# Pair products of 32 fields: stores of three pairs in 12 KB rows, weights in whole 128-partition blocks of six pairs

## The chip, the cores and the metric

One core of one Trainium2 chip. The metric is the device time of one execution in microseconds (us), taken from several runs; the profile is of one execution, and its span is about 1.8 us shorter than that execution's time (768.7 us for the profiled one of the kernel before, 2 us above the median). The times of the kernels told here may be compared.

## The reference

For every pair of fields i < j (496 pairs of 32 fields) the row of field i goes through the pair's own 128x128 matrix and is multiplied by the row of field j:

```python
v_i = inputs[:, I_IDX, :]                            # 1024 x 496 x 128, fp32
v_j = inputs[:, J_IDX, :]
transformed = jnp.einsum('bpd,ped->bpe', v_i, W)     # W: 496 x 128 x 128
return transformed * v_j                             # 1024 x 496 x 128 = 260 MB
```

## The kernel before

Embedding lies on the 128 partitions and the batch of 1024 along the row; the host transposes. A "half-pair" is 512 columns of one pair. TensorE makes its product in PSUM: one fp32 matmul for the first 15 pairs, three matmuls of split operands (h, l, d) for the rest, with ScalarE scaling PSUM between them. ScalarE and GpSimd split weights and x. VectorE multiplies PSUM by field j into an output tile. SyncE issues nearly all transfers, loads and stores, in the order of the program.

```python
WL = 8          # pairs in one block of weights
OG = 2          # pairs in one output tile, and in one store
rpool = ctx.enter_context(tc.tile_pool(name="wr", bufs=3))   # raw weights, 4 KB a partition
opool = ctx.enter_context(tc.tile_pool(name="o", bufs=4))    # output, 8 KB a partition
...
def load_w(c, half, splits=(0, WL)):
    ...
        nc.sync.dma_start(out=w_raw[c][half::2, a:b, :], in_=wt[c, half, :, a:b, :])
...
def second(u):                                   # of half-pair u = 2 q + h
    ...
    g, k = divmod(q, OG)
    if k == 0 and h == 0:
        ots[g] = opool.tile([P, OG, BT], F32, tag="ot", name=f"ot_{g}")
    nc.vector.tensor_tensor(ots[g][:, k, s], po.pop(u), x_sb[j][:, s], ALU.mult)
    if q >= NQ - 2:
        nc.sync.dma_start(out=out[g, :, k, s], in_=ots[g][:, k, s])
    elif k == OG - 1 and h == 1:
        nc.sync.dma_start(out=out[g], in_=ots[g])

for u in range(2 * NQ + LAG):
    q = u // 2
    if u % (2 * WL) == 4 and (q // WL + 2) * WL < NQ:
        load_w(q // WL + 2, 1)                   # every second partition of a block
    if u % (2 * WL) == 12 and (q // WL + 3) * WL < NQ:
        load_w(q // WL + 3, 0)                   # the other ones, four pairs later
    ...
```

What matters later: the weights go out as two transfers of 64 partitions each (4 packets for each of the 16 DMA engines), four pairs apart, with two stores between them.

Of the kernel before, what the change touches and what calls it, by code (L numbers as in the profile page):

```python
# [7 lines left out]
F32 = mybir.dt.float32  # L8
# [3 lines left out]
P = 128  # L12
NF = 32
NQ = NF * (NF - 1) // 2
BT = 1024
HB = 512
WC = 2
WL = 8
OG = 2
EPS = 2.0**-12  # L20
NATIVE = 5
SHARED = 10
XDLAG = 10
LAG = 3
XLEAD = 5


def _pairs():

    return [(i, j) for i in range(NF - 2, -1, -1) for j in range(i + 1, NF)]  # L30


@with_exitstack
def kernel(
    ctx: ExitStack,
    tc: tile.TileContext,
    xt: bass.AP,
    wt: bass.AP,
    out: bass.AP,
):  # L40
















    nc = tc.nc
    pairs = _pairs()
    nchunk = NQ // WC

    xpool = ctx.enter_context(tc.tile_pool(name="x", bufs=1))
    spool = ctx.enter_context(tc.tile_pool(name="xs", bufs=2))
    rpool = ctx.enter_context(tc.tile_pool(name="wr", bufs=3))
    wpool = ctx.enter_context(tc.tile_pool(name="ws", bufs=4))
    opool = ctx.enter_context(tc.tile_pool(name="o", bufs=4))
    ppool = ctx.enter_context(tc.tile_pool(name="ps", bufs=8, space=bass.MemoryType.PSUM))

    x_sb = {}

    def load_x(f, n=1, pieces=1, eng=None):  # L70

        t = xpool.tile([P, n, BT], F32, tag=f"x{f}", name=f"x_{f}")
        s = BT // pieces
        for k in range(pieces):
            (eng or nc.sync).dma_start(out=t[:, :, k * s : (k + 1) * s], in_=xt[:, f : f + n, k * s : (k + 1) * s])
        for k in range(n):
            x_sb[f + k] = t[:, k, :]

    w_raw = {}

    def load_w(c, half, splits=(0, WL)):

        if c not in w_raw:
            w_raw[c] = rpool.tile([P, WL, P], F32, tag="w", name=f"w_{c}")
        for a, b in zip(splits, splits[1:]):
            nc.sync.dma_start(out=w_raw[c][half::2, a:b, :], in_=wt[c, half, :, a:b, :])

    w_s = {}

    def split_w(c, u):  # L90

        k = c * WC % WL
        raw = w_raw[c * WC // WL][:, k : k + WC, :].rearrange("p q e -> p (q e)")
        h, l, d = [wpool.tile([P, WC * P], F32R, tag=t, name=f"{t}_{c}") for t in ("wh", "wl", "wd")]
        nc.scalar.mul(h, raw, 1.0 - 2.0**-13)  # L95
        nc.gpsimd.tensor_tensor(l, raw, h.bitcast(F32), ALU.subtract)  # L96
        nc.gpsimd.tensor_scalar(d, h.bitcast(F32), EPS, 1.0, ALU.mult, ALU.mult)  # L97
        nc.gpsimd.tensor_tensor(d, l.bitcast(F32), d.bitcast(F32), ALU.subtract)  # L98
        w_s[c] = (h, l, d)

    x_s = {}
    later = []

    def split_x(f, a, u):

        if a == 0:
            x_s[f] = [spool.tile([P, BT], F32R, tag=t, name=f"{t}_{f}") for t in ("xh", "xl", "xd")]
        s = slice(a, a + HB)
        h, l, d = [t[:, s] for t in x_s[f]]
        nc.scalar.mul(h, x_sb[f][:, s], 1.0 - 2.0**-13)  # L110
        nc.gpsimd.tensor_tensor(l, x_sb[f][:, s], h.bitcast(F32), ALU.subtract)  # L111
        nc.gpsimd.tensor_scalar(l, l.bitcast(F32), 1.0 / EPS, 1.0, ALU.mult, ALU.mult)  # L112
        if f > NF - 2 - NATIVE - SHARED:
            later.append((min(u + XDLAG, 2 * first_q[f] + LAG - 1), d, h.bitcast(F32), l.bitcast(F32)))
        else:
            nc.gpsimd.tensor_tensor(d, h.bitcast(F32), l.bitcast(F32), ALU.subtract)  # L116

    nq0 = NATIVE * (NATIVE + 1) // 2
    c0 = nq0 // WC
    first_q = {i: q for q, (i, j) in reversed(list(enumerate(pairs)))}  # L120



    todo = []
    for c in range(c0, nchunk):
        todo.append(((c - 3) * WC + 1, max(c * WC, nq0), lambda u, c=c: split_w(c, u)))
    for i in range(NF - 2 - NATIVE, -1, -1):
        for a in range(0, BT, HB):
            todo.append((first_q[i + 1] + 1 if i < NF - 3 - NATIVE else 2, first_q[i], lambda u, i=i, a=a: split_x(i, a, u)))
    todo.sort(key=lambda t: t[1])  # L130

    load_w(0, 0, (0, 1))
    load_w(0, 1, (0, 1))
    load_w(0, 0, (1, WL))
    load_w(0, 1, (1, WL))
    load_x(NF - 2, pieces=2, eng=nc.scalar)
    load_x(NF - 1, pieces=2, eng=nc.scalar)
    load_x(NF - 3)
    load_x(NF - 4)
    load_w(1, 0)  # L140
    for f in range(NF - 5, NF - 4 - XLEAD, -1):
        load_x(f)
    load_w(1, 1)
    load_w(2, 0)


    ctx.enter_context(tc.manual_schedule())
    po, ots = {}, {}


    def first(u):
        q, h = divmod(u, 2)
        i, c = pairs[q][0], q // WC
        r = slice(q % WC * P, (q % WC + 1) * P)
        s = slice(h * HB, (h + 1) * HB)
        po[u] = ppool.tile([P, HB], F32, tag="po", name=f"po_{u}")
        if q < nq0:
            nc.tensor.matmul(po[u], w_raw[q // WL][:, q % WL, :], x_sb[i][:, s], start=True, stop=True)  # L158
        else:
            for t in (0, 1):  # L160
                nc.tensor.matmul(po[u], w_s[c][t][:, r], x_s[i][t][:, s], start=t == 0, stop=t == 1)  # L161
            nc.scalar.mul(po[u], po[u], 1.0 + EPS)  # L162

    def second(u):
        q, h = divmod(u, 2)
        i, j = pairs[q]
        r = slice(q % WC * P, (q % WC + 1) * P)
        s = slice(h * HB, (h + 1) * HB)
        if q >= nq0:
            nc.tensor.matmul(  # L170
                po[u], w_s[q // WC][2][:, r], x_s[i][2][:, s], start=False, stop=True, skip_group_check=True
# [4 lines that stand above are left out]
        nc.vector.tensor_tensor(ots[g][:, k, s], po.pop(u), x_sb[j][:, s], ALU.mult)  # L176
        if q >= NQ - 2:
            nc.sync.dma_start(out=out[g, :, k, s], in_=ots[g][:, k, s])
        elif k == OG - 1 and h == 1:
            nc.sync.dma_start(out=out[g], in_=ots[g])  # L180

    for u in range(2 * NQ + LAG):
        q = u // 2
        if u % (2 * WL) == 4 and (q // WL + 2) * WL < NQ:
            load_w(q // WL + 2, 1)
        if u % (2 * WL) == 12 and (q // WL + 3) * WL < NQ:
            load_w(q // WL + 3, 0)
        if u < 2 * NQ:
            i, j = pairs[q]
            if u % 2 == 0 and j == i + 1 and 0 <= i - 2 - XLEAD:  # L190
                load_x(i - 2 - XLEAD)
            first(u)
        if u >= LAG:
            second(u - LAG)
        if u % 2 == 1:
            ready = [t for t in todo if t[0] <= q]
            if ready:
                ready[0][2](u)
                todo.remove(ready[0])
        while later and later[0][0] <= u:  # L200
            nc.vector.tensor_tensor(*later.pop(0)[1:], ALU.subtract)  # L201
    assert not todo and not later
# [27 lines left out]
```

## Time and profile before

| | before |
|---|---|
| time, median of 3 runs | 766.5 us (765.69 to 768.17) |
| SyncE's queue | 50,544 packets, 98.9% of 16 engines' span |
| stores / weight loads / x loads on that queue | 251 / 126 / 30 transfers |
| TensorE, the next busiest | 93% |

The lines behind this are in the prediction. The kernel is bound by DMA, so the account is one of a DMA engine's time, worked out from the packet records of the trace and averaged over the 16 engines:

- *net*: for each size of packet, the count times the median duration, less the 3 ns by which a packet overlaps its follower;
- *stalls*: what packets took above the median of their size, for stores and for loads apart;
- *gaps*: time between packets in which the engine had none; *rest*: fetches of instructions (2.2 to 2.5), the start, the run-out and the lag of the slowest engine.

Before: 726.0 net + 14.2 stalls of stores + 10.4 of loads + 7.1 gaps + 9.1 rest = 766.8, the span. A *ring* is here the queue that one issuing engine (SyncE or ScalarE) fills; *landing* is the last of a transfer's sixteen semaphore updates.

### The profile page before, as it was taken

How to read it: one execution, taken by the hardware profiler on the slowest of the kernel's cores; microseconds unless marked ns; L12 is line 12 of the kernel's file. 1: busy time of each engine (PE TensorE's matmuls, PEld its weight loads, DVE VectorE, ACT ScalarE, POOL GpSimd, SP SyncE). 2: the span in 40 equal slices, each digit the busy share in tenths (PEclk: the TensorE clock that was granted, in tenths of full speed). 3: DMA queues.
4: the chain of work that ended last, by engine and by line, in shares of the span. 5: the costliest groups of instructions: out<-in, count | busy, mean ns of one | idle time of the engine just before them, and what ended most of it. 6: DMA issues, size and time to landing. Idle time of an engine off the chain costs nothing.

```text
span 766.8 us, 11879 instructions
## 1 busy us (share of the span) xinstructions
PE 715.1 (93%) x2946; PEld 547.0 (71%) x2946; DVE 631.9 (82%) x1012; ACT 634.0 (83%) x1256; POOL 594.8 (78%) x863
## 2 busy tenths in 40 slices
PE   6997999999999998999999989999999999999994
PEld 2475776677767676777776768787878777777773
DVE  3878988898877787887787878888888888888895
ACT  2186988888888898888888989998989899999893
POOL 1687998879889878878788786979787879696660
PEclk9999999999999999999999999999999999999997
DMA  9999999999999999999999999999999999999997
GB/s 341 397 419 406 414 406 385 412 397 410 415 407 409 409 393 413 410 414 413 392 424 408 401 398 405 418 414 418 418 419 421 413 408 416 410 410 411 409 399 294
DMA packets 51189, 310.12 MB, mean 404 GB/s; under 512 B 6576, under 2 KB 6704, under 8 KB 19504
## 3 DMA queue, kind: packets, MB, share of 16 engines
q1 hardware_dynamic: 50544, 308.31, 98.9%
q10 hardware_dynamic: 576, 1.05, 0.4%
q8 instruction: 24, 0.39, 0.2%
q14 instruction: 45, 0.37, 0.1%
HBM read 49.28 MB, written 260.05 MB: 403 GB/s over the span
## 4 chain that ended last, share of the span: by engine, by line
DMA 45%; PE 33%; DVE 17%; issue 2%; POOL 1%; DVEq 0%; ACT 0%; ACTq 0%; POOLq 0%
DMA out_dram<-ot 44%; PE po L161 21%; DVE ot L176 16%; PE po L170 10%; PE po L158 2%; DVE xd L201 2%; DMA x<-in_xt_dram 1%; POOL xd L116 0%; POOL xl L111 0%; POOL wl L96 0%; DVEq L176 0%; POOL wd L98 0%; POOL xl L112 0%; ACT wh L95 0%; POOL wd L97 0%
## 5 line engine op out<-in xcount | busy, mean ns | idle before, releaser
L176 DVE TENSOR_TENSOR ot<-po,x 128x512 f32<-128x512 f32 x992 | 618.6, 684 | 126.0 <-DMA out_dram<-ot 76.3
L162 ACT ACTIVATE po<-po 128x512 f32<-128x512 f32 x962 | 550.5, 583 | 103.8 <-PE po L161 56.2
L161 PE MATMUL po<-xh,wh 128*128 128x512 f32 x962 | 386.8, 402 | 26.0 <-DVE ot L176 25.0
L170 PE MATMUL po<-xd,wd 128*128 128x512 f32 x962 | 377.0, 392 | 5.4 <-DVE xd L201 4.5
L161 PE MATMUL po<-xl,wl 128*128 128x512 f32 x962 | 377.8, 393 | 3.4 <-POOL wl L96 3.4
L161 PEld LDWEIGHTS po<-xh,wh 128*128 128x128 f32 x962 | 181.1, 188 | 101.5 <-DVE ot L176 63.3
L96 POOL TENSOR_TENSOR wl<-w,wh 128x256 fp32r<-128x256 f32 x241 | 180.2, 748 | 87.0 <-ACT wh L95 77.2
L170 PEld LDWEIGHTS po<-xd,wd 128*128 128x128 f32 x962 | 181.4, 189 | 46.1 <-ACT po L162 5.2
L161 PEld LDWEIGHTS po<-xl,wl 128*128 128x128 f32 x962 | 181.4, 189 | 38.2 <-POOL wl L96 5.4
L98 POOL TENSOR_TENSOR wd<-wl,wd 128x256 fp32r<-128x256 f32 x241 | 179.9, 746 | 20.1
L97 POOL TENSOR_SCALAR wd<-wh 128x256 fp32r<-128x256 f32 x241 | 99.8, 414 | 20.3
L95 ACT ACTIVATE wh<-w 128x256 fp32r<-128x256 f32 x241 | 99.2, 412 | 3.1 <-DMA w<-in_wt_dram 3.1
L111 POOL TENSOR_TENSOR xl<-x,xh 128x512 fp32r<-128x512 f32 x52 | 67.5, 1298 | 19.7 <-ACT xh L110 19.5
L116 POOL TENSOR_TENSOR xd<-xh,xl 128x512 fp32r<-128x512 f32 x32 | 41.4, 1294 | 2.7
L110 ACT ACTIVATE xh<-x 128x512 fp32r<-128x512 f32 x52 | 32.5, 629 | 11.5 <-DMA x<-in_xt_dram 11.4
L112 POOL TENSOR_SCALAR xl<-xl 128x512 fp32r<-128x512 f32 x52 | 32.6, 628 | 4.6
L158 PE MATMUL po<-x,w 128*128 128x512 f32 x60 | 30.1, 664 | 6.0 <-DMA w<-in_wt_dram 5.0
L158 PEld LDWEIGHTS po<-x,w 128*128 128x128 f32 x60 | 12.5, 212 | 22.7 <-issue 18.8
L201 DVE TENSOR_TENSOR xd<-xh,xl 128x512 fp32r<-128x512 f32 x20 | 16.5, 826 | 0.0
L110 ACT ACT_TABLE_LOAD x1 | 1.3, 1283 | 2.7 <-issue 2.7
L217 POOL MEMSET const-float32-0.0<- 128x1 f32 x1 | 0.1, 98 | 0.2 <-issue 0.2
L217 POOL MEMSET const-bfloat16-1.0<- 128x1 bf16 x1 | 0.1, 101 | 0.0
(2 smaller groups left out, 0.2 us busy)
## 6 DMA issues: line engine op xcount, KB each, us to landing
out_dram<-ot SPq DMA_DIRECT2D x247, 1024.0 KB, 8.9
w<-in_wt_dram SPq DMA_DIRECT2D x122, 256.0 KB, 9.1
x<-in_xt_dram SPq DMA_DIRECT2D x30, 512.0 KB, 8.8
x<-in_xt_dram ACTq DMA_DIRECT2D x4, 256.0 KB, 4.0
out_dram<-ot SPq DMA_DIRECT2D x4, 256.0 KB, 7.3
w<-in_wt_dram SPq DMA_DIRECT2D x2, 224.0 KB, 5.5
w<-in_wt_dram SPq DMA_DIRECT2D x2, 32.0 KB, 3.2
```

What stands on the lines that cost most here:

```text
L95: nc.scalar.mul(h, raw, 1.0 - 2.0**-13)
L96: nc.gpsimd.tensor_tensor(l, raw, h.bitcast(F32), ALU.subtract)
L97: nc.gpsimd.tensor_scalar(d, h.bitcast(F32), EPS, 1.0, ALU.mult, ALU.mult)
L98: nc.gpsimd.tensor_tensor(d, l.bitcast(F32), d.bitcast(F32), ALU.subtract)
L110: nc.scalar.mul(h, x_sb[f][:, s], 1.0 - 2.0**-13)
L111: nc.gpsimd.tensor_tensor(l, x_sb[f][:, s], h.bitcast(F32), ALU.subtract)
L116: nc.gpsimd.tensor_tensor(d, h.bitcast(F32), l.bitcast(F32), ALU.subtract)
L158: nc.tensor.matmul(po[u], w_raw[q // WL][:, q % WL, :], x_sb[i][:, s], start=True, stop=True)
L161: nc.tensor.matmul(po[u], w_s[c][t][:, r], x_s[i][t][:, s], start=t == 0, stop=t == 1)
L162: nc.scalar.mul(po[u], po[u], 1.0 + EPS)
L170: nc.tensor.matmul(po[u], w_s[q // WC][2][:, r], x_s[i][2][:, s], start=False, stop=True, skip_group_check=True)
L176: nc.vector.tensor_tensor(ots[g][:, k, s], po.pop(u), x_sb[j][:, s], ALU.mult)
```

## The change

Intent: fewer, longer packets and a deeper output pool. A tile holds three pairs, a row of a store has 12 KB, and four tiles hold twelve pairs in place of eight. Four tiles of 12 KB need 48 KB a partition, and beside the old weights the build says that 47.6 KB are left, so the raw weights shrink from 4 KB rows to 3 KB rows (six pairs), and both halves of a block become one transfer of all 128 partitions.

```diff
-WL = 8
-OG = 2
+WL = 6
+OG = 3
+WB = 3
+WLEAD = 9
...
+    def load_w(c, splits=(0, WL)):
+        w_raw[c] = rpool.tile([P, WL, P], F32, tag="w", name=f"w_{c}")
...
-            nc.sync.dma_start(out=w_raw[c][half::2, a:b, :], in_=wt[c, half, :, a:b, :])
+            nc.sync.dma_start(out=w_raw[c][:, a:b, :], in_=wt[c, :, a:b, :])
...
+    w_at = {}
+    for c in range(WB, -(-NQ // WL)):
+        free = (c - WB + 1) * WL if (c - WB) * WL < nq0 else 0
+        w_at[max(c * WL - 3 * WC + 1 - WLEAD, free)] = c
...
+        elif g == 0 or q >= NQ - 1 - OG:
+            if h == 1:
+                nc.sync.dma_start(out=out[g, :, k], in_=ots[g][:, k])
         elif k == OG - 1 and h == 1:
             nc.sync.dma_start(out=out[g], in_=ots[g])
...
-        if u % (2 * WL) == 4 and (q // WL + 2) * WL < NQ:
-            load_w(q // WL + 2, 1)
-        if u % (2 * WL) == 12 and (q // WL + 3) * WL < NQ:
-            load_w(q // WL + 3, 0)
+        if u % 2 == 0 and q in w_at:
+            load_w(w_at[q])
```

The host's layouts of weights and output follow (cut). No compute instruction changes.

More of the change, by code (lines that the diff above doesn't have):

```diff
@@ L62 @@
     spool = ctx.enter_context(tc.tile_pool(name="xs", bufs=2))
-    rpool = ctx.enter_context(tc.tile_pool(name="wr", bufs=3))
+    rpool = ctx.enter_context(tc.tile_pool(name="wr", bufs=WB))
     wpool = ctx.enter_context(tc.tile_pool(name="ws", bufs=4))
@@ L79 @@
     w_raw = {}
-    def load_w(c, half, splits=(0, WL)):
-        if c not in w_raw:
-            w_raw[c] = rpool.tile([P, WL, P], F32, tag="w", name=f"w_{c}")
+    def load_w(c, splits=(0, WL)):
+        w_raw[c] = rpool.tile([P, WL, P], F32, tag="w", name=f"w_{c}")
         for a, b in zip(splits, splits[1:]):
-            nc.sync.dma_start(out=w_raw[c][half::2, a:b, :], in_=wt[c, half, :, a:b, :])
+            b = min(b, NQ - c * WL)
+            nc.sync.dma_start(out=w_raw[c][:, a:b, :], in_=wt[c, :, a:b, :])
     w_s = {}
@@ L130 @@
     todo.sort(key=lambda t: t[1])
-    load_w(0, 0, (0, 1))
-    load_w(0, 1, (0, 1))
-    load_w(0, 0, (1, WL))
-    load_w(0, 1, (1, WL))
+    load_w(0, (0, 1, WL))
     load_x(NF - 2, pieces=2, eng=nc.scalar)
@@ L139 @@
     load_x(NF - 4)
-    load_w(1, 0)
+    load_w(1)
     for f in range(NF - 5, NF - 4 - XLEAD, -1):
         load_x(f)
-    load_w(1, 1)
-    load_w(2, 0)
+    load_w(2)
+    w_at = {}
+    for c in range(WB, -(-NQ // WL)):
+        free = (c - WB + 1) * WL if (c - WB) * WL < nq0 else 0
+        w_at[max(c * WL - 3 * WC + 1 - WLEAD, free)] = c
     ctx.enter_context(tc.manual_schedule())
@@ L214 @@
     xt = _np.ascontiguousarray(x.transpose(2, 1, 0))
-    wt = _np.ascontiguousarray(w[perm].reshape(NQ // WL, WL, P, P // 2, 2).transpose(0, 4, 3, 1, 2))
+    nload = -(-NQ // WL)
+    wt = _np.zeros((nload * WL, P, P), _np.float32)
+    wt[:NQ] = w[perm]
+    wt = _np.ascontiguousarray(wt.reshape(nload, WL, P, P).transpose(0, 3, 1, 2))
     nc = _bacc.Bacc("TRN2", target_bir_lowering=False, num_devices=1, dynamic_dma_scratch_size=256)
@@ L221 @@
         args.append(nc.dram_tensor(f"in_{name}_dram", a.shape, mybir.dt.from_np(a.dtype), kind="ExternalInput").ap())
-    args.append(nc.dram_tensor("out_0_dram", (NQ // OG, P, OG, BT), F32, kind="ExternalOutput").ap())
+    args.append(nc.dram_tensor("out_0_dram", (-(-NQ // OG), P, OG, BT), F32, kind="ExternalOutput").ap())
     with tile.TileContext(nc) as tc:
@@ L227 @@
     y = _np.empty((BT, NQ, P), _np.float32)
-    y[:, perm, :] = got.transpose(3, 0, 2, 1).reshape(BT, NQ, P)
+    y[:, perm, :] = got.transpose(3, 0, 2, 1).reshape(BT, -1, P)[:, :NQ]
     return y
```

## The prediction

> **What bounds the kernel now.** I read the busy shares first, then the DMA queues, then a table by stage, then the waits, and last the records of single DMA packets. The page's head:
>
> ```profile
> span 766.8 us, 11879 instructions
> PE 715.1 (93%) x2946; PEld 547.0 (71%) x2946; DVE 631.9 (82%) x1012; ACT 634.0 (83%) x1256; POOL 594.8 (78%) x863
> ...
> DMA  9999999999999999999999999999999999999997
> ...
> q1 hardware_dynamic: 50544, 308.31, 98.9%
> ...
> HBM read 49.28 MB, written 260.05 MB: 403 GB/s over the span
> ```
>
> No compute engine is full, and the DMA engines are in the nines in 39 of 40 slices. The one queue that SyncE fills takes 98.9% of 16 engines' span. So the time is that of moving 308 MB; 260 MB of it is output and can't shrink. The table by stage (busy of PE, PEld, DVE, ACT, POOL; clock; DMA share; GB/s) tells whether the ends differ, and how far TensorE is behind the DMA:
>
> ```profile
> 0.00:40.00 40.00, 34.05 (x79) 16.09 (x80) 23.58 (x36) 8.06 (x16) 16.51 (x24) 1.00 0.96 372
> 300.00:500.00 200.00, 190.32 (x804) 147.20 (x803) 165.71 (x269) 175.49 (x347) 162.05 (x236) 1.00 1.00 408
> 500.00:700.00 200.00, 196.38 (x843) 155.99 (x842) 173.86 (x281) 181.49 (x362) 162.60 (x243) 1.00 1.01 414
> 740.00:767.00 27.00, 15.72 (x69) 12.46 (x67) 17.35 (x28) 13.59 (x26) 6.58 (x11) 0.83 0.79 318
> ```
>
> The DMA is full in the middle; the two ends lose 1.6 us (0.04 x 40) and 5.7 us (0.21 x 27), part of the second being shares that overlap or the run-out after the last store. PE reaches 98% of the 500-to-700 stretch, so it is the next bound there. How near it is, the timeline of PE tells:
>
> ```profile
> 37.04 0.39 PE L161 MATMUL po<-xl,wl 128*128 128x512 f32 x1
> 37.27 0.39 PE L161 MATMUL po<-xh,wh 128*128 128x512 f32 x1
> 37.49 0.39 PE L161 MATMUL po<-xl,wl 128*128 128x512 f32 x1
> 37.72 0.39 PE L170 MATMUL po<-xd,wd 128*128 128x512 f32 x1
> ```
>
> Matmuls start 0.228 us apart, so one half-pair (three of them) needs 0.683 us. The 500-to-700 window has 281 VectorE half-pairs, 0.712 us each: PE has 4% in hand there. Over the kernel it needs 962 x 0.683 = 657 us, plus about 33 us of start and the first 30 pairs' halves in fp32: some 690 us, well under 766.
>
> Then who waits, and for what (microseconds in total, times, longest):
>
> ```profile
> DVE ot L176 <- DMA out_dram<-ot: 76.3, 93, 2.6
> SPq L180 <- DVE ot L176: 436.0, 244, 4.0
> SPq L86 <- POOL wd L98: 26.0, 26, 1.3
> ```
>
> VectorE waits for output tiles to be stored: this is back-pressure of a full DMA, and it costs nothing by itself. SyncE waits for VectorE because it issues in order; with transfers landing about 9 us after issue, its queue normally holds three transfers:
>
> ```profile
> out_dram<-ot SPq DMA_DIRECT2D x247, 1024.0 KB, 8.9
> w<-in_wt_dram SPq DMA_DIRECT2D x122, 256.0 KB, 9.1
> x<-in_xt_dram SPq DMA_DIRECT2D x30, 512.0 KB, 8.8
> ```
>
> **The packets.** The trace lists every packet with size and time. On SyncE's queue 31,616 packets of 8192 B have a median of 309 ns (mean 316), 11,648 of 4096 B a median of 159 (mean 172), and 6,512 of 4 B (the semaphore of each transfer on each of 16 engines) 9 ns. Following packets of one engine in time, starts are 306 ns apart for 8192 B, 155 for 4096 B and 6 for the semaphore: a packet overlaps its follower by some 3 ns. So a packet costs 2 x 155 - 306 = 4 ns, about 4.5 with rounding, whatever its size, and the bytes run at 4096/150.5 = 27.2 GB/s an engine, 435 for sixteen. The means above the medians are stalls[...]: 7 ns x 31,616 / 16 = 14 us for the stores, 13 ns x 11,648 / 16 = 10 us for the loads.
>
> The sixteen semaphore updates of one transfer tell something more: they are not together. In the late stretch thirteen engines land a 1 MB store within 4 to 5 us of its issue, the last one after 8.9. Engines that lead run out of issued work, seen as pauses of 0.4 to 0.6 us at 121, 372, 420, 457, 608 and 740 us that end 0.85 us after the next store's issue. Gaps between packets sum to about 7 us an engine, 1 of them in the first 6 us. The slowest engine has the fewest of them and sets the landing.
>
> **What the Trainium skill says.** "DMA: Bandwidth & Descriptors", section "Why small descriptors are slow (HBM only)", gives a fixed overhead of about 3 cycles a packet inside the DMA engine; at the 850 MHz of its section "Where 436 GB/s comes from" that is 3.5 ns, and the ceiling is 435 GB/s for 16 engines. The trace agrees with both: 4 to 4.5 ns, and 435 GB/s from 150.5 ns for 4096 B. The same page, section "Rules for kernel authors", asks for 128 partitions and 1 MiB or more in a transfer and says that splitting a transfer in two partition halves gains nothing, as both use the same engines. The weight loads before are such halves (every second partition); no run yet shows what joining them is worth.
>
> **The change, part by part.**
> 1. Stores. Before: 247 transfers of 128 rows of 8 KB and four of 128 rows of 2 KB, 32,128 packets. After: 496 pairs are 163 whole groups of three (489 pairs), five single pairs (0, 1, 2, 492, 493) and two pairs in halves: 163 x 128 = 20,864 packets of 12 KB, 640 of 4 KB, 512 of 2 KB: 22,016. That is 10,112 fewer, 632 an engine, x 4.5 ns = -2.8 us. I expect a 12 KB row to stay one packet, as 16 KB packets stand in the trace (instruction fetches), at 309 + 150 = 459 ns.
> 2. Weights. Before 126 transfers of 64 rows, 8,064 packets. After 83 blocks, the first split in two: 84 x 128 = 10,752. That is 2,688 more, 168 an engine: +0.8 us.
> 3. Semaphores. 407 transfers on this queue become 163 + 5 + 4 + 84 + 30 = 286: 121 fewer an engine x 6 ns = -0.7 us.
> The page's count should fall from 50,544 to 20,864 + 640 + 512 + 10,752 + 3,840 + 4,576 = 41,184. Sum of the fixed costs: -2.7 us (with the overlapping 9 ns a packet it would be 585 x 9 = 5.3, an upper bound). All of it lies on the bounding resource.
> 4. Buffers. Four tiles of three pairs hold 12 pairs in place of 8. VectorE and PE may run further ahead, and engines that lead may run further before they dry up. This pays only where the slow engine is not always the same: of the some 6 us of gaps I take -1.5 us.
> 5. Load stalls. Loads have 13 ns of stall each on average, 23 for the first after a semaphore. 42 fewer load transfers and full 128-partition rows should take some off, more and shorter rows put some on: -1 us.
> 6. Start. First pairs stored singly go out earlier, but the queue is then full of loads (the first store issued at 15.5 us begins to move at 19), so nothing; two weight issues fewer bring the first x loads some 1.2 us forward: -0.3 us. End: the last stores remain halves, nothing.
> Compute is the same instructions on every engine; no tile shape changes.
> Sum: 766.5 - 2.7 - 1.5 - 1.0 - 0.3 = 761.0 us.
>
> **Rivals.**
> - Fuller pipe: the larger pool ends nearly all gaps and halves the stalls of loads. Then -2.7 - 6 - 5: about 753. For: the gaps are there and the landings spread by 4 to 5 us. Against: the landing of the slowest engine is what VectorE waits for, and a deeper pool gives that engine no less to do. Pauses of leaders are a symptom, not the bound.
> - PE takes over in the last 300 us, where it has 4% in hand and no x loads are left. It would cap the gain at some 10 us there; my gain is 0.7%, so it shouldn't show except as a higher PE share. It speaks against anything near 745.
> - Late weights: a load now waits behind up to four stores of 1.5 MB. At 9 us for about three transfers of 1 MB before, I expect 12 to 14 for the median after. It is issued some 11 pairs ahead of its use by ScalarE, 11 x 1.42 us = 16 us. If the slowest engine takes more than that, ScalarE, then PE, then VectorE stall by some microseconds a time. Three full output tiles behind it keep the DMA busy, so I give this +0 to +5 us: 762 to 767.
> - Rows of 12 KB are cut in pieces or stall more a byte: packets stay near 50,000 and nothing is gained: 766 to 768.
>
> **Range and chances.** The known part is small (2.7 us) and sure; the others are each 1 to 2 us and could go either way, and a run's median scatters by 1 us. 80%: 754 to 767. Faster by over 2% needs under 751.2, which takes the whole first rival and more: 5%. Slower by over 2% (over 781.8) needs real starvation by late weights or SyncE held up in front of a load: 2%. Within 2%: 93%.
>
> **What would show it.** Step 1 right: packets of 41,184 on that queue and a 12 KB median near 459 ns; wrong if 12 KB takes over 470 or is split. Steps 2, 5: 3 KB loads with a median near 121 ns and a mean under 134. Step 4: VectorE's wait for stores falls below 76 us though the DMA share stays at 98 to 99%; if gaps vanish and the time falls by over 8 us, the first rival was right. Late weights would show as ScalarE waiting for the weight DMA (3.1 us before) and DMA digits of 8 in the middle. A DMA share under 97% in the middle stages would make the prediction wrong in its base.

## The result, and the profile after

The changed kernel takes 771.24 us (median of six runs, 769.92 to 773.48), the kernel before 766.45 (six runs, 765.18 to 768.17). The ratio is 1.0062, with a 95% interval of 1.0041 to 1.0083: same within 2%, but slower, and outside the predicted 754 to 767. (A ratio here is the mean time of one kernel's runs over that of the other's of the same rounds, so not quite the ratio of the medians that I quote.) The profiled run is the slowest of the six; that of the kernel before is as far above its median, so the two profiles may be compared.

In the numbering of the changed kernel L179 is VectorE's multiply, L186 the stores and L87 the weight loads (L176, L180 and L86 before). From the page of the changed kernel (section 6's columns: transfers, KB each, median us from issue to landing):

```profile
span 771.7 us, 11499 instructions
PE 713.8 (92%) x2946; PEld 549.6 (71%) x2946; DVE 629.0 (82%) x1012; ACT 632.2 (82%) x1256; POOL 593.7 (77%) x863
...
GB/s 353 427 421 423 420 422 397 393 393 390 392 398 415 395 380 400 399 413 392 404 390 416 408 395 402 411 414 415 413 407 403 419 413 415 400 412 411 412 399 288
DMA packets 41825, 310.08 MB, mean 402 GB/s; under 512 B 4640, under 2 KB 4768, under 8 KB 20896
...
q1 hardware_dynamic: 41184, 308.30, 98.5%
...
out_dram<-ot SPq DMA_DIRECT2D x163, 1536.0 KB, 13.7
w<-in_wt_dram SPq DMA_DIRECT2D x81, 384.0 KB, 14.1
```

The packets fell to 41,184, the predicted number to the last digit, and the bytes are the same. The queue is still busy for 98.5% of the span. So fewer packets kept the engines busy for longer: the mean time of a packet rose by more than its bytes. The GB/s row shows where: 420 to 427 in slices 2 to 6, then 380 to 419 up to the run-out. The page of the kernel before has, for comparison:

```profile
GB/s 341 397 419 406 414 406 385 412 397 410 415 407 409 409 393 413 410 414 413 392 424 408 401 398 405 418 414 418 418 419 421 413 408 416 410 410 411 409 399 294
```

The stages of the changed kernel (busy of PE, PEld, DVE, ACT, POOL with instructions in brackets; clock; DMA share; GB/s):

```profile
0.00:40.00 40.00, 35.85 (x93) 18.46 (x94) 27.30 (x42) 11.12 (x22) 18.66 (x28) 1.00 0.97 391
100.00:300.00 200.00, 183.26 (x759) 141.69 (x758) 163.26 (x261) 166.16 (x333) 165.38 (x237) 0.98 1.00 398
300.00:500.00 200.00, 188.13 (x794) 147.78 (x793) 163.28 (x266) 172.18 (x342) 159.74 (x233) 0.99 0.99 402
500.00:700.00 200.00, 195.50 (x835) 154.67 (x834) 170.19 (x279) 180.43 (x357) 161.32 (x239) 1.00 1.01 410
740.00:772.00 32.00, 17.20 (x75) 13.57 (x73) 18.54 (x31) 14.71 (x28) 7.54 (x12) 0.82 0.79 324
```

And the one stage of the kernel before that the prediction did not show:

```profile
100.00:300.00 200.00, 185.81 (x774) 143.11 (x773) 166.32 (x267) 170.15 (x340) 171.46 (x244) 0.99 1.00 405
```

The start gained (391 GB/s for 372, 42 VectorE instructions for 36 in the first 40 us). From 100 to 700 us every stage lost 4 to 7 GB/s, at a DMA share that stayed at 0.99 or more. That is the signature of slow packets, not of missing work. The waits of the changed kernel (us in total, times, longest), first VectorE and ScalarE:

```profile
DVE ot L179 <- DMA out_dram<-ot: 71.7, 60, 3.5
...
ACT wh L96 <- DMA w<-in_wt_dram: 8.5, 3, 7.9
```

then SyncE:

```profile
SPq L186 <- DVE ot L179: 524.0, 162, 5.7
SPq L87 <- POOL wl L97: 31.2, 19, 3.6
```

VectorE's wait for stores fell below the 76 us of before, as step 4 of the prediction has it, without any gain in time. ScalarE waited for weights three times, 8.5 us in all, so late weights are not the cause. SyncE was held in front of weight loads by GpSimd still reading the raw tile (three such lines, 74 us in all; the longest is shown). Does that delay the stores behind? I compared, for each store, the issue with the end of VectorE's work on its tile: all delays above 0.3 us sum to 5.4 us in the whole kernel (11.7 before). It does not.

The account of an engine's time says what grew (I also count *doubled* store packets, those that took more than 1.8 times the median of their size):

| us of an engine | before | after | difference |
|---|---|---|---|
| net packet time | 726.0 | 723.2 | -2.8 |
| stalls of stores | 14.2 | 26.3 | +12.1 |
| stalls of loads | 10.4 | 4.2 | -6.2 |
| gaps | 7.1 | 8.1 | +1.0 |
| rest | 9.1 | 9.8 | +0.7 |
| span (sum, rounded) | 766.8 | 771.7 | +4.9 |
| doubled store packets | 322 | 488 | +166 |

A 12 KB packet has a median of 460 ns and a mean of 480; an 8 KB packet had 309 and 316. The packet that costs the time is thus a store that stalls, and the question is what makes it stall.

### The profile page after: what moved, and what is told of

The parts are those of the page before. It is cut to its first block, busy times and chain, and to the rows that moved or that the text cites. A ratio compares the mean times of both kernels' runs of the same rounds, so it can differ in the third digit from the quotient of the medians. Undisturbed runs are those within 1.5% of the kernel's fastest.

```text
span 771.7 us, 11499 instructions
## 1 busy us (share of the span) xinstructions
PE 713.8 (92%) x2946; PEld 549.6 (71%) x2946; DVE 629.0 (82%) x1012; ACT 632.2 (82%) x1256; POOL 593.7 (77%) x863
## 3 DMA queue, kind: packets, MB, share of 16 engines
q1 hardware_dynamic: 41184, 308.30, 98.5%
## 4 chain that ended last, share of the span: by engine, by line
DMA 61%; DVE 18%; PE 18%; issue 1%; DVEq 0%; POOL 0%; ACT 0%; POOLq 0%
DMA out_dram<-ot 61%; DVE ot L179 17%; PE po L164 9%; PE po L173 4%; PE po L161 4%; DVE xd L205 1%; DMA x<-in_xt_dram 0%; DVEq L179 0%; POOL xd L117 0%; ACT wh L96 0%; POOL wl L97 0%; ACT po L165 0%; DVEq L230 0%; POOLq L97 0%
## 5 line engine op out<-in xcount | busy, mean ns | idle before, releaser
L179 DVE TENSOR_TENSOR ot<-po,x 128x512 f32<-128x512 f32 x992 | 615.4, 683 | 130.8 <-DMA out_dram<-ot 71.7
L164 PE MATMUL po<-xl,wl 128*128 128x512 f32 x962 | 379.4, 394 | 10.9 <-POOL wl L97 9.7
## 6 DMA issues: line engine op xcount, KB each, us to landing
w<-in_wt_dram SPq DMA_DIRECT2D x81, 384.0 KB, 14.1
x<-in_xt_dram SPq DMA_DIRECT2D x30, 512.0 KB, 14.2
out_dram<-ot SPq DMA_DIRECT2D x4, 256.0 KB, 10.2
```

The source lines that it names most:

```text
L164: nc.tensor.matmul(po[u], w_s[c][t][:, r], x_s[i][t][:, s], start=t == 0, stop=t == 1)
```

## The experiments

Three theories, and what each stands on:

- **W**, the weights: one block of 128 partitions puts eight load packets behind each other on each engine where there had been four and four with two stores between; the stores around that burst stall.
- **R**, the rows: a 12 KB row by itself stalls more a byte.
- **D**, depth: more stores queued means more stalls, or late weights.

The stores alone (12 KB rows with the old weights) would be the first thing to run, but four tiles of 12 KB with them don't fit, as said above, nor do six tiles of 8 KB. So the parts are taken from the other side: new weights with old stores.

### The weights alone, then depth

**e1_weights_alone**: from the changed kernel, tiles of two pairs as before. (A condition for the last single pairs is reworded too, here and in e2 to e7, e10, e12 and e15 to e17.)

```diff
-OG = 3
+OG = 2
```

> The changed weights (3 KB rows, 128 partitions, one transfer per six pairs) with the old stores: two pairs, 8 KB rows, four tiles. What is known: in the changed kernel the loads' stalls above the median fell from 9.6 to about 4 us an engine, the stores' rose from 14.2 to 26.3, and five engines land some 7 us after the other eleven. Theory R (the 12 KB row itself stalls more): stores' excess stays at 14 us, the loads' falls to about 4, so some 5 us faster than before: 760 to 763. Theory D (deeper output buffers let engines drift apart, and the drift costs): the same, 760 to 763, landings spread under 5 us. Theory W (loads in 128 partitions push their stalls onto the stores): stores' excess 22 us or more, time 768 to 773.

Measured: 778.08 us, ratio 1.0146 (1.0122 to 1.0169): slower than all three theories had it. The weights alone cost 11.5 us, so the stores of three pairs gave about 7 back. Stalls of stores 20.6 us (14.2 before; W had asked for 22), and 661 doubled packets of 8 KB (322): rows of 12 KB are not needed for it. W stands, R as the sole cause falls. The stalls of loads, which all three theories had falling to about 4 us, rose to 12.6 (10.4 before): their fall in the changed kernel isn't the new weights' doing alone.

**e2_six_tiles_8k**: e1 with six tiles, the same 48 KB of output as four tiles of 12 KB.

```diff
-    opool = ctx.enter_context(tc.tile_pool(name="o", bufs=4))
+    opool = ctx.enter_context(tc.tile_pool(name="o", bufs=6))
```

> As the run with the weights alone, but six tiles of two pairs: the same 12 pairs of output buffer as the changed kernel, in 8 KB rows. Theory R: stores' excess about 14 us, time as with the weights alone or a little less, 758 to 763. Theory D: the five late engines come back, spread 6 to 8 us, stores' excess 22 us or more, time 769 to 773.

Measured: 769.03 us, ratio 1.0027 (1.0005 to 1.0048), 9 us faster than e1. Depth helps; D as "depth hurts" falls. (The time lies in the range written for D, but that range took e1 to be at 760 to 763. The late engines did come back, as D had it: the landings of one store, from the first engine to the last, spread over 9.8 us in the median, 4.8 in e1, for stores of 300 to 720 us. The spread doesn't set the time: it is 7.8 in the changed kernel and 7.7 in e18, the fastest run below.) But the run isn't clean as a measure of rows, because a new wait came, ScalarE for weights:

```profile
ACT wh L96 <- DMA w<-in_wt_dram: 81.7, 59, 10.1
```

**e3_three_tiles_12k**: the changed kernel with three tiles (nine pairs, about the depth of before).

```diff
-    opool = ctx.enter_context(tc.tile_pool(name="o", bufs=4))
+    opool = ctx.enter_context(tc.tile_pool(name="o", bufs=3))
```

> The changed kernel with three tiles of three pairs in place of four: 9 pairs of output buffer (before: 8), rows still 12 KB. Theory R: stores' excess stays at 24 us or more, time 769 to 775. Theory D: spread falls to about 4 us, excess to 14 to 18 us, time 759 to 764.

Measured: 789.56 us, ratio 1.0298 (1.0274 to 1.0322), slower than either theory had it. The fourth tile is worth 18 us. Stalls of stores are 37.3 us, gaps 14.8. With less queued, one stall is easy to find. The timeline of SyncE in this kernel (start, us, instruction):

```profile
642.79 1.15 SPq L87 DMA_DIRECT2D w<-in_wt_dram  x1
646.64 4.93 SPq L186 DMA_DIRECT2D out_dram<-ot  x2
651.66 1.12 SPq L87 DMA_DIRECT2D w<-in_wt_dram  x1
```

and the windows of 1.6 us around what follows (last two columns: DMA share, GB/s):

```profile
644.40:646.00 1.60, 1.60 (x9) 1.31 (x8) 1.60 (x4) 1.37 (x4) 1.23 (x3) 1.00 0.97 415
646.00:647.60 1.60, 1.60 (x9) 1.31 (x8) 0.69 (x3) 1.49 (x4) 0.74 (x2) 1.00 1.03 300
...
653.60:655.20 1.60, 1.60 (x9) 1.31 (x8) 1.60 (x4) 1.38 (x3) 1.43 (x3) 1.00 1.07 438
655.20:656.80 1.60, 1.60 (x9) 1.24 (x7) 0.68 (x2) 1.50 (x4) 1.51 (x2) 1.00 0.82 234
```

One dip follows each of these two weight loads, some 3.5 us after its issue. In the first the share is 1.03 at 300 GB/s, so the engines are busy and slow; in the second the share is 0.82, so a part of that dip is idle time. The packet records in steps of 0.4 us say that the slow packets are those of the store ahead of the block, not of the block (slow: over 1.4 times the median):

```
from us   GB/s
 645.6    430
 646.0    387    8 store packets slow, 1 of them doubled
 646.4    337
 646.8    280   10 store packets slow, 8 of them doubled
 647.2    253
 647.6    309   26 load packets start
 648.0    416   49 load packets start
 649.2    429
```

So eight to ten of the sixteen engines slow at once, for about 1.6 us, just before the first of them reaches the load. Nor is it this load alone. Packets can be assigned to engines by their starts and ends, and then 709 of this kernel's 758 doubled store packets are among the last two packets that their engine has in front of a load (of weights or x), where only 14% of all store packets stand. It is 408 of 488 in the changed kernel, and 257 of 322 in the kernel before. Why a store slows then, the trace doesn't say.

### What of the block is it: row, width or burst?

**e5_halves_together**: e1 with the block again as two transfers of 64 partitions, issued back to back.

```diff
-            nc.sync.dma_start(out=w_raw[c][:, a:b, :], in_=wt[c, :, a:b, :])
+            for half in halves:                      # (0, 1)
+                nc.sync.dma_start(out=w_raw[c][half::2, a:b, :], in_=wt[c, half, :, a:b, :])
```

> As the run with the weights alone (778.1 us), but each block of six pairs is loaded in two transfers of 64 partitions (every second one, as before), one right after the other. Seen so far: in the run with the weights alone and in the one with three tiles, DMA falls from 430 to 250 GB/s for about 1.6 us once per weight load, in the last two store packets that most engines have in front of it; those packets take twice their time. Theory A (a burst of eight load packets an engine with nothing queued behind it stalls the stores in front): the burst is the same, 775 to 780. Theory B (3 KB rows against 4 KB): 775 to 780. Theory C (128 partitions at once against 64): 764 to 769.

Measured: 778.94 us (776.0 to 781.9), ratio 1.016 (1.0112 to 1.0208), as slow as e1 (at 2% the verdict is unclear). It is not the number of partitions in a transfer.

**e6_halves_apart**: the same two transfers three pairs apart, with a fourth raw tile to make room for that.

```diff
-WB = 3
+WB = 4
...
-        w_at[max(c * WL - 3 * WC + 1 - WLEAD, free)] = c
+        at = max(c * WL - 3 * WC + 1 - WLEAD, free + 3)
+        w_at[at - 3], w_at[at] = (c, (0,)), (c, (1,))
```

> As the one before, but the two halves are issued three pairs apart, as in the kernel before (there four pairs apart), with a fourth raw weight tile so that the first half can go earlier. Theory A: bursts of four packets, 763 to 769 and the doubled 8 KB packets (656 in the run with the weights alone, 320 in the kernel before) fall to about 320. Theory B: 775 to 780. Theory C: 764 to 769.

Measured: 767.22 us, ratio 0.9999 (0.9974 to 1.0024). The whole cost of the weights is gone, 11.7 us of e5, with the same packets and the same bytes; doubled packets fall from 924 to 454. In the account of the two, 9.5 of the 9.6 us between the profiled spans are stalls of stores (27.8 and 18.3). The fourth raw tile comes with it, and e5 with a fourth raw tile was not run, so the pair is not perfectly clean. The lateness of stores behind held loads doesn't explain it: it is 44.7 us in sum in e5, 21.2 in e6, but 5.4 in e1, which is as slow as e5.

**e7_whole_of_eight**: e1 with blocks of eight pairs, rows of 4 KB as before, still whole.

```diff
-WL = 6
+WL = 8
```

> As the run with the weights alone, but blocks of eight pairs, so 4 KB rows as in the kernel before, still 128 partitions in one transfer. Theory A: the burst is eight packets as well, but comes 62 times and not 83: 773 to 779. Theory B: 764 to 769. Theory C: 775 to 780.

Measured: 773.02 us, ratio 1.0066 (1.0031 to 1.0101). The long row doesn't bring the old time back, so the row is not the whole cause. By the ratios, each against the kernel before in its own rounds, e7 has some 45% of e1's cost (0.0066 of 0.0146), where 62 blocks in place of 83 would leave 75%. So the number of bursts alone doesn't account for the difference, and a part that comes with the 3 KB row is not excluded.

**e8_before_five_tiles**: the kernel before with five output tiles.

```diff
-    opool = ctx.enter_context(tc.tile_pool(name="o", bufs=4))
+    opool = ctx.enter_context(tc.tile_pool(name="o", bufs=5))
```

> The kernel before with five output tiles in place of four, nothing else: what depth of output buffer alone is worth with the old weights. If depth helps by keeping work queued behind the loads (theory A): 760 to 764, doubled packets under 250, pauses of the leading engines shorter. If depth helped only against the new weights' form: 765 to 768.

Measured: 766.57 us, ratio 0.9989 (0.9963 to 1.0014). Where the halves are spread, depth is worth nothing. I take it from this that what depth earned in e2, and from e3 to the changed kernel, was cover against the bursts; that is argued, not measured by itself.

### The same in the changed kernel: spread, pitch, and another ring

**e4_pitch_16k**: the changed kernel with rows of the output 16 KB apart in memory, a test of R: if 12 KB at a pitch of 12 KB is an unlucky layout, this mends it.

```diff
-    args.append(nc.dram_tensor("out_0_dram", (-(-NQ // OG), P, OG, BT), F32, kind="ExternalOutput").ap())
+    args.append(nc.dram_tensor("out_0_dram", (-(-NQ // OG), P, 4, BT), F32, kind="ExternalOutput").ap())
...
-            nc.sync.dma_start(out=out[g], in_=ots[g])
+            nc.sync.dma_start(out=out[g, :, :OG], in_=ots[g])
```

> The changed kernel, but each 12 KB row of the output starts 16 KB after the one before in HBM (4 KB unused between them). Theory R in the form that it is where the rows lie (a pitch of 12 KB puts several engines on the same part of HBM): the five late engines go or change in number, time moves by over 3 us either way. R in the form that it is the packet's length, and theory D: no change, 769 to 773, five engines late by 7 us.

Measured: 765.44 us, ratio 0.9981 (0.9961 to 1.0), 5.8 us faster than the changed kernel. But stalls of stores fell only from 26.3 to 23.6; gaps fell from 8.1 to 3.1. The five late engines stay (five land over 5 us after the first in the median store). Something of R is in it, in the form of where the rows lie, and I come back to it with e15.

**e9_changed_halves_apart** and **e10_pitch_halves_apart**: e6's spreading in the changed kernel and in e4, with three raw tiles (a fourth doesn't fit). The edit is that of e6 without `WB = 4`.

> The changed kernel (12 KB rows, four tiles) with one edit: each block of six pairs' weights goes in two transfers of 64 partitions, three pairs apart, so that one store lies between them; three raw weight tiles as in the change. Theory A (the burst of eight load packets an engine is what the change lost): the doubled 12 KB packets fall from 488 to under 300, and the time from 771.2 to 760 to 765, under the kernel before; the prediction's saving on packets is then seen. Rival (12 KB rows at a 12 KB pitch are what costs, the weights only with few tiles): 769 to 772.

> As the one before, with the output rows 16 KB apart in HBM as in the run of that name (765.4 us with whole blocks). Theory A: both gains add up, 757 to 762. Rival (the pitch took away the same stalls, so nothing is left to gain): 764 to 767.

Measured: 771.36 us, ratio 1.0074 (1.0035 to 1.0113), and 769.91, ratio 1.0047 (1.0008 to 1.0085). Neither gained; e9 lies in its rival's range, e10 above both of its ranges. Yet the doubled packets fell from 488 to 266, and from 453 to 303; stalls of stores in e9 are 16.7 us. What ate it is, as I read it, a new wait. SyncE's waits in e9:

```profile
SPq L89 <- POOL wd L100: 242.7, 73, 7.5
```

The first half is now issued before GpSimd has done with its raw tile, SyncE stands there and the stores behind it go out late (84.7 us summed over the stores, 5.4 in the changed kernel); gaps rise to 11.1 us.

**e13_halves_one_store_apart**: halves one pair apart, so that the tile is free.

```diff
+        at = max(c * WL - 3 * WC + 1 - WLEAD, free)
+        w_at[at], w_at[at + 1] = (c, (0,)), (c, (1,))
```

> The changed kernel with weights in two transfers of 64 partitions, the first where the whole block is issued now, the second one store (three pairs) later, so that SyncE waits no longer than in the changed kernel. If the burst is the loss: stores late after VectorE under 20 us in all, doubled 12 KB packets under 300, 760 to 766. If it isn't: 769 to 773. A rival that would hide it: the second half has 3 pairs less lead, and ScalarE waits for weights by over 40 us.

Measured: 770.10 us, ratio 1.0051 (1.0009 to 1.0092). The stores are on time (12.5 us of lateness), doubled packets are 298 (though stalls of stores are still 22.7 us), but now the second half lands late, the rival that had been written down, which the waits of ScalarE show:

```profile
ACT wh L98 <- DMA w<-in_wt_dram: 66.4, 53, 8.9
```

So spreading removes doubled packets in the changed kernel as well, but no run of it shows what that is worth in time. **e12_six_tiles_halves_apart**, e2 with the same spreading, went the same way:

> As the first of this group (halves apart) with two pairs a tile and six tiles: the same 12 pairs of buffer, in 8 KB rows. If the row's length costs nothing beyond its packets, 163 x 128 packets of 12 KB against 246 x 128 of 8 KB are 10,600 fewer, 665 an engine x 4.5 ns = 3 us: this one is 2 to 4 us slower than with 12 KB rows. If 12 KB rows stall more: this one is the same or faster, 757 to 763.

Measured: 770.43 us, ratio 1.005 (1.0025 to 1.0075); its stores go out 327 us late in sum, and ScalarE waits 81.5 us for weights; 214 us of SyncE's waits are for earlier stores to land. Many small transfers meet a limit: no trace here shows more than eight transfers in flight. The traces tell where it comes from: all transfers of a kernel, of both issuing engines, take eight semaphores of the program in turn, and an issue waits until the earlier transfer on its semaphore has landed (in the changed kernel 252 of the 253 semaphore waits that stand right before an issue of SyncE are for the issue's own semaphore). So it is a limit of how the program was built. Whether the chip would take more, no run tells, and the run tells little about the rows.

**e11_weights_on_act_queue** takes the loads out of the stores' ring in place of spreading them: the changed kernel, with its blocks of weights from the fourth on issued by ScalarE, at the same place of the program.

```diff
-            nc.sync.dma_start(out=w_raw[c][:, a:b, :], in_=wt[c, :, a:b, :])
+            (nc.scalar if c >= WB else nc.sync).dma_start(out=w_raw[c][:, a:b, :], in_=wt[c, :, a:b, :])
```

> The changed kernel with the weight loads from the fourth block on issued by ScalarE, so that they stand in its own ring and the DMA engines alternate between them and the stores. Theory A in its narrow form (the load stands in the stores' own ring, with nothing behind it): doubled 12 KB packets under 250, 758 to 766. Wide form (eight HBM reads an engine at once slow the stores wherever they stand): doubled packets 400 or more, 768 to 774. ScalarE has 132 us idle and needs some 81 x 0.5 = 40 us for issuing, so it should not become the bound.

Measured: 759.46 us (759.35 to 762.69), ratio 0.9915 (0.9885 to 0.9946): 11.8 us faster than the changed kernel, with the same packets, rows, tiles and order of stores (against the kernel before it is the same within 2%, but faster). The page shows the loads in a queue of their own and landing sooner (8.7 us for 14.1):

```profile
q1 hardware_dynamic: 29664, 276.97, 88.5%
q10 hardware_dynamic: 12096, 32.38, 11.0%
...
w<-in_wt_dram ACTq DMA_DIRECT2D x79, 384.0 KB, 8.7
```

The stages of e11, against those of the changed kernel above:

```profile
100.00:300.00 200.00, 190.21 (x789) 144.52 (x788) 166.49 (x272) 173.58 (x345) 170.98 (x244) 1.00 1.01 418
300.00:500.00 200.00, 192.75 (x811) 149.64 (x810) 165.48 (x270) 176.85 (x351) 163.17 (x238) 1.00 1.01 412
500.00:700.00 200.00, 195.60 (x834) 154.26 (x832) 169.56 (x277) 180.60 (x357) 160.94 (x240) 1.00 1.01 410
```

398 became 418 GB/s and 402 became 412; from 500 us on nothing is gained, where PE stands at 98% and has little more to give. In the account, stalls of stores are 16.1 us (26.3), of loads 5.2 (4.2), gaps 2.2 (8.1), rest 10.9 (9.8): -10.2 + 1.0 - 5.9 + 1.1 = -14.0, the difference of the two profiled spans (the changed kernel's profiled run is its slowest, so the medians differ by less). Doubled packets are 278 (488; the expectation had asked for under 250). The burst itself is broken up: of the weight packets 79% pass an engine in unbroken runs of eight in the changed kernel, 33% in e11, where another 32% pass singly between packets of stores. Could it be SyncE, no longer held at loads, that brings the gain? It waits for landings of weights instead (44.7 us), and the stores are late by 14.7 us in sum, 5.4 in the changed kernel: no. The 12 KB rows are the same, so R falls as the main cause (a part of a few us may be left to it: stalls of stores are 16.1 us here and 13.2 in e16 below, at the same depth with 8 KB rows): the burst of loads in the stores' own ring cost about 12 us in the changed kernel, as it did in e1. That the gaps shrink because engines that lead find more work is my reading, not shown.

**e15_pitch_weights_on_act**: e4 and e11 together.

> The run with the weights on ScalarE's ring, with output rows 16 KB apart in HBM. If where the rows lie costs by itself: 753 to 757. If the pitch only helped against the burst: 758 to 762.

Measured: 762.63 us (760.1 to 765.5), ratio 0.9941 (0.9905 to 0.9977); it overlaps e11's range. With the loads out of the ring the pitch gains nothing, so it isn't a cost of 12 KB rows by themselves. What it did in e4 stays unexplained.

**e17_e1_weights_on_act**, **e16_six_tiles_weights_on_act** and **e14_before_weights_on_act**: e11's one line in e1, in e2 and (for both halves of a block from the fourth on) in the kernel before.

> The run with the weights alone (8 KB rows, four tiles, whole blocks of six pairs; 778.1 us, stores' stalls 20.6, loads' 12.6, gaps 8.6 us an engine) with the loads from the fourth block on issued by ScalarE. If loads in the stores' ring are the cost: stores' stalls about 15, 762 to 768. If it is the short buffers (four tiles, eight pairs) that let any read burst through: over 772, stalls about as they were.

> The run with the weights on ScalarE's ring, with six tiles of two pairs in 8 KB rows. By the packets' fixed cost it is 3 us slower than with 12 KB rows: 761 to 764. If 12 KB rows stall more than they save: 755 to 759. Late weights should be gone (81.7 us of ScalarE's waits in the run with six tiles and one ring).

> The kernel before (8 KB rows, four tiles, halves of eight pairs) with the weight loads from the fourth block on issued by ScalarE. If loads standing in the stores' ring cost in every kernel: 758 to 763. If only whole bursts of eight packets do (half transfers were fine already): 764 to 768; then the change on top of this ring is worth the 5 to 8 us to e11's 759.5.

Measured: e17 771.35 us (766.4 to 774.6), ratio 1.0043 (0.9995 to 1.0092), 6.7 us faster than e1, between its two ranges, with stalls of stores down from 20.6 to 11.7 but gaps up from 8.6 to 12.4; what these gaps come from stays open. e16 770.00, ratio 1.0029 (1.0002 to 1.0057), no gain over e2. e14 773.05, ratio 1.0079 (1.0045 to 1.0113), 6 us slower than before. Both are slower than all that was expected of them. SyncE's waits, of e16 and then of e14, name what came instead:

```profile
SPq L186 <- DMA w<-in_wt_dram: 190.8, 35, 9.8
```

```profile
SPq L180 <- DMA w<-in_wt_dram: 86.6, 45, 9.6
```

A store waits there for a load of the other ring to land before it may be issued (264 us of lateness of stores in e16, 43 in e14). With stores of 1 MB there are more transfers, and as all share the eight semaphores the turn of an old load comes sooner. With 1.5 MB stores (e11) the lateness is 14.7 us. So another ring is no remedy by itself: in these runs it paid where the loads come in bursts, and most where the transfers are few.

**e18_all_loads_on_act**: e11 with the x loads of the steady part moved as well.

```diff
-                load_x(i - 2 - XLEAD)
+                load_x(i - 2 - XLEAD, eng=nc.scalar)
```

> The changed kernel with all steady loads, weights and x, issued by ScalarE, so that SyncE's ring holds stores alone after the start. If x loads cost in the ring as the weights did: stores' stalls from 16.1 to about 12 us in the first 465 us, 755 to 759 in all. If not: 758 to 763, as e11.

Measured: 759.09 us (758.73 to 759.25), ratio 0.9891 (0.9849 to 0.9932); one of the eleven runs of the kernel before took 776.2 us in these rounds, and by the medians the ratio is 0.9905. It is the best version here, with the changed kernel's stores and weights, and beats both kernels; against e11 it is no more than level, but its six runs lie within 0.5 us. The budgets of the runs (an engine's time of the profiled run, us):

| | net | stalls stores | stalls loads | gaps | doubled | median time |
|---|---|---|---|---|---|---|
| before | 726.0 | 14.2 | 10.4 | 7.1 | 322 | 766.5 |
| e1 weights alone | 726.6 | 20.6 | 12.6 | 8.6 | 661 | 778.1 |
| e5 halves together | 726.8 | 27.8 | 6.5 | about 6 | 924 | 778.9 |
| e6 its halves apart | 726.8 | 18.3 | 6.7 | 5.0 | 454 | 767.2 |
| changed kernel | 723.2 | 26.3 | 4.2 | 8.1 | 488 | 771.2 |
| e11 its weights in ScalarE's queue | 723.1 | 16.1 | 5.2 | 2.2 | 278 | 759.5 |
| e18 x loads there too | 723.1 | 15.1 | 4.8 | 3.8 | 206 | 759.1 |

## Why the prediction was wrong

- **What bounds the kernel**: right. The queue is at 98.5%, and PE did not become the bound (92%).
- **Steps 1 to 3, packets**: right. 41,184 packets, 12 KB in one piece at a median of 460 ns, 3 KB at 121; net packet time fell by 2.8 us, where 2.7 were predicted.
- **Step 5, stalls: the step that failed.** The prediction read the stores' 14 us of stalls in the view of packets and gave them no term in the sum; it gave the loads -1. Measured: stores +12.1, loads -6.2, together +5.9. Behind it stands the belief, in step 5, that "full 128-partition rows should take some off". Loads did stall less, and stores stalled more by about twice that. The sign that it had named for this step, 3 KB loads with a mean under 134 ns, came true (122.6), but it looked at loads alone; and the loads' gain was no merit of the reasoning, as with the joined blocks alone they stalled more (12.6 us in e1, where the mean of 3 KB loads is 134.5 ns). The stores' trouble stood in the trace of the kernel before: 257 of its 322 doubled packets are among the last two in front of a load. The sign of the joined halves was wrong: e1 shows them at +11.5 us by themselves, e6 shows that spreading takes it back, and e11 shows about 12 us in the changed kernel itself.
- **Step 4, buffers**: -1.5 predicted for gaps, +1.0 measured. The tiles of three pairs did pay, some 7 us of the weights' 11.5 (e1 against the changed kernel). Of that 3.4 us are net packet time, which steps 1 to 3 had; the rest is, as I read it, cover against the bursts, which is not how the step argued: with spread halves a fifth tile is worth nothing (e8).
- **Step 6, start**: the first 40 us did gain, 391 for 372 GB/s; it doesn't decide anything.
- **The rivals**: PE did not take over. Late weights did not come in the changed kernel (8.5 us) but did in e2 and e13, so the margin was thin. Of the last one, "stall more a byte" came true in the mean, 480 ns, though the limit of 470 was written for the median, which is 460; its cause, the row, was not the main one (e11 has the same rows and 10 us less of it). The fuller pipe at 753 did not come; what took most of the gaps away, in e11, was the queue of the loads and not the pool.

The sum of the account closes: -2.8 + 12.1 - 6.2 + 1.0 + 0.7 = +4.8, against a span that grew by 4.9.

What stays open: why stores ahead of a burst of loads take twice their time; why the pitch of 16 KB helped only with whole blocks of loads in the same ring; whether a fourth raw tile alone has a part in what e6 gained; and what 12 KB rows are worth in time against 8 KB at one depth, since the runs meant for it (e2, e12, e16) had waits of their own, in which the eight semaphores have a part.

## What to carry to other kernels

In a kernel bound by DMA, count not only packets and bytes but what each packet takes above its median, for stores and loads apart, before and after; a share of 98% hides it. Where loads share a ring with a full stream of stores, try them in small portions spread between the stores, or from a second issuing engine, and either way look at what the issuing engine then waits for: here each of the two won about 12 us once (e6, e11), and each also met a new wait and won nothing (e9, e16). And give a cost that you have read from the profile a term in the sum, even where you think it stays as it is.

## What the Trainium skill lacked or had wrong

- "DMA: Bandwidth & Descriptors", section "Rules for kernel authors", says of two transfers to partition halves that they aren't worth it and asks for one of 128 partitions. Back to back that agrees (e5 778.9, e1 778.1 us); three pairs apart in a stream of stores, with a fourth raw tile, the halves took 767.2 us (e6). The row should say so.
- The same page, section "Issuing engines are not separate DMA queues", and the same table say that spreading transfers over issuing engines doesn't raise bandwidth. Here the loads from ScalarE took the changed kernel from 771.2 to 759.5 us (e11) at equal bytes and packets, 398 to 418 GB/s in the stage of 100 to 300 us. It is no rule the other way: in the kernel before it cost 6 us (e14).
- The fixed overhead of a packet in its section "Why small descriptors are slow (HBM only)" is about 3 cycles; the prediction's 3.5 ns for it is an estimate at the page's 850 MHz, and the packets show 4 to 4.5. With that the sum held: 632 store packets an engine fewer, 168 load packets more and 121 semaphores fewer give 464 x 4.5 ns + 121 x 6 ns = 2.8 us, and 2.8 were measured.
- No page has the stall of stores in front of a burst of loads: 1.6 us at 300 GB/s in place of 415 in one dip of e3, at 234 in place of 438 in the next (a part of that idle), and 709 of e3's 758 doubled packets among the last two before a load.
- No page gives a size for the drift of the sixteen engines within one transfer. Landings of one late store (issued at 713.7, 708.0 and 724.5 us), in us after the first engine, from the traces:

```
before        0.0 0.2 0.2 0.2 0.3 0.3 0.4 0.5 0.6 0.7 0.7 0.8 0.9 1.2 1.3 4.8
changed       0.0 0.0 0.1 0.1 0.1 0.2 0.2 0.2 0.5 0.8 1.0 7.1 7.1 7.2 7.3 7.7
e11           0.0 0.0 0.1 0.1 0.1 0.1 0.1 0.1 0.1 0.2 0.5 1.0 1.0 1.0 1.2 7.3
```

- No page says that the number of semaphores that a program's transfers take in turn limits the transfers in flight: eight here, in every trace, and 190.8 us of SyncE's waits for older loads in e16.
